# Attention by the two-level scheme of layer 1: exp(a) v as (exp(a) h) Wv^T in a graph-attention kernel

## The chip, the cores and the metric

The kernel runs on one core of one Trainium2 chip. The metric is the device time of one execution in microseconds, the median of several. A core has five engines, each with its own instruction queue: TensorE (PE, matrix products; its weight loads are listed as PEld), VectorE (DVE), ScalarE (ACT), GpSimd (POOL) and SyncE (SP), which here only issues loads. They meet through semaphores. Transfers run beside them; SP issues the loads and POOL the stores.

## The reference, cut to what matters

```python
h = maximum(layernorm(x), 0)                       # x: 3327 x 512, adj: 3327 x 3327
q, k, v = h @ Wq.T + bq, h @ Wk.T + bk, h @ Wv.T + bv
a = q @ k.T / sqrt(512) + adj + adj
x = x + softmax(a) @ v                             # layer 0
h = maximum(layernorm(x), 0)
A2 = adj + eye
temp = A2 @ h @ W.T
d = diagonal(A2) ** -0.5
out = x + relu((d[:, None] * A2 * d[None, :]) @ temp)   # layer 1
```

All of it is in fp32. So there are four large products: the scores, exp(a) with v, A2 with h, and A2 with temp. The rows are padded to 26 tiles of 128.

## The kernel before, in words

All large products are made by a recursive scheme of Strassen's kind (Winograd's form): a 2 x 2 block product in seven products instead of eight, with four sums of blocks of the left matrix (`four_sums`, L169) and four differences of the right one (`four_differences`, L175). The upper and lower half of the nodes are 13 tiles each (`HALF`); `STRIPS` and `HT` cut the columns into a strip of 2 x 7 tiles (s = 0) and one of 2 x 6 tiles (s = 1); the half widths `Q` are 448 and 384. On-chip memory is one arena of named slots (`large`, `mid`, `half`, `quarter`), which `ring` hands out in turn. A tile whose slot was used before waits until the last reader of the old one is done, a store's landing among them.

**Prologue.** M = Wq^T Wk is made on PE (L293). `h_transposed` (L309) normalises tiles of x, applies relu on ACT, transposes them on PE and keeps h^T with its sums in `hp`, four packs of 3, 3, 3 and 4 tile pairs (`PACKS`). `project_q` (L329) and `project_v` (L360) make q and v of a pack by one level of the scheme and store them in memory, POOL issuing. `Chain` (L223) writes the seven products of one level so that each partial result is evicted from its PSUM bank while others run; the last product, p4, of a chain runs after the fourth product (p6) of the next.

**Scores.** 52 steps: four groups of columns (strip s, half q), 13 tile pairs t in each. A step loads four quarter blocks of adj^T into `g` (`adjacency`, L428), runs a `Chain` of 28 PE records with DVE adding each product to 2 adj (`first`, `more`, L477 and L482), lets ACT take exp (`settle`, L470) and stores the four blocks of exp in `pd`. Beside the evictions `outer_sums` (L438) makes the next step's four sums of A2 = adj + 1 for layer 1 and stores them in `sumd`. `in_order` (L122) holds DVE, PE, POOL and SP to the order of the program text in this stage; elsewhere Tile's scheduler orders the instructions.

**Attention.** 91 units (L615 on): for two row tiles of the result at a time and each t, `weights` loads exp blocks, `four_sums` makes their sums, DVE adds up the row sums, and 7 x 2 products of width 256 with the blocks of v go into seven banks (L634). At t = 12 `attend` (L565) takes the row sums by small matmuls with `ones` (L573), puts the seven products together, divides, adds x, stores x1, normalises and stores h of layer 1 in `rowd`.

**Layer 1.** Two passes g = 0 and 1 (A2 with h, A2 with temp) by two levels of the scheme. The outer level is seven products in turn (`ORDER`: p5, p1, p6, p7, p2, p3, p4), each for two strips, in steps t = 0 to 5, which take two tile pairs each, and a last one with the odd tile (`t is None`). `left` (L720) loads the outer block or sum of A2 (from `adjT` or `sumd`), `sums` makes the four inner sums on DVE, `Right` loads and combines the right-hand rows (`load` 7 steps ahead, `make` 4 ahead), `multiply` (L798) issues 7 matmuls of width 448 or 384 (L810; L802 for the odd tile), and `gather` puts a product's result into `cts`. After a product's sums for a tile are complete, `temp` (L864, 4 matmuls of width 512, L869) multiplies with W, and `finish` writes the output. `between` names what else is put after which step. The five slots of `a_ring` let `left` run ahead.

Of the kernel before, what the change touches and what calls it, by code (L numbers as in the profile page):

```python
# [15 lines left out]
P = 128  # L16
# [28 lines left out]
def graph_layers_kernel(  # L45
# [26 lines left out]

    nc = tc.nc
# [30 lines left out]

    def quarter(k, shape, name):
        return arena.tile(shape, F32, name=name, tag=f"quarter{k}")
# [53 lines left out]

    qd = dram.tile([P, DC, NP], F32, name="qd")
    vd = [dram.tile([P, 4, E], F32, name=f"vd{t}") for t in range(HALF)]
    pd = [[dram.tile([P, 4, H[s]], F32, name=f"p{s}_{t}") for t in range(HALF)] for s in range(2)]
    sumd = [[dram.tile([P, len(SUMS), H[s]], F32, name=f"sum{s}_{t}") for t in range(HALF)] for s in range(2)]
    x1d = [dram.tile([P, D], F32, name=f"x1d{i}") for i in range(NT)]
    rowd = [[dram.tile([P, D], F32, name=f"row{g}_{i}") for i in range(NT)] for g in range(2)]
    t2d = [[dram.tile([P, 4, P], F32, name=f"t2{g}_{t}") for t in range(PAIRS + 1)] for g in range(2)]
# [38 lines left out]
    PACKS = ((0, 3), (3, 3), (6, 3), (9, 4))  # L206
# [55 lines left out]
    x_ring = ring(*((mid, k) for k in (0, 1, 2, 5)))  # L262
    v_ring = ring(*((mid, k) for k in (9, 10, 11, 12, 3, 6, 7, 8)))
# [5 lines left out]

    order = [(k, t + y * HALF) for k, (a, n) in enumerate(PACKS) for t in range(a, a + n) for y in range(2)]  # L270
    first = {i: load_x(i, nc.scalar) for _, i in order[:4]}
# [9 lines left out]
    bv_sb = quarter(0, [P, D], "bv_sb")  # L281
    nc.sync.dma_start(bv_sb, bass.AP(tensor=bv.tensor, offset=bv.offset, ap=[[0, P], [1, D]]))
    w_v = blocks(range(8, 12), "wv")
    for c in range(DC):
        for z in range(2):
            nc.sync.dma_start(w_v[2 * (c // 2) + z][:, c % 2], wvT[c * P : (c + 1) * P, z * E : (z + 1) * E])
# [17 lines left out]
    for b in (M, w_v):  # L304
        for _ in four_differences(b):
            pass
        nc.scalar.mul(b[0], b[0], -1.0)

    def h_transposed(k):  # L309

        a, n = PACKS[k]
        for _, i in (o for o in order if o[0] == k):
            xt = first.pop(i) if i in first else load_x(i)
            rstd, nb = norm(xt)
            nc.scalar.activation(xt, xt, AF.Relu, bias=nb, scale=rstd)
            pt = tp_bank("tp").rearrange("p (c e) -> p c e", c=DC)
            for c in range(DC):
                nc.tensor.transpose(pt[:, c], xt[:, c * P : (c + 1) * P], ident)  # L318
# [10 lines left out]
    def project_q(k):  # L329
# [3 lines left out]
        qs = [half(12 + j, [P, 2, BW], "qs") for j in range(4)]  # L333
# [26 lines left out]
    def project_v(k):  # L360
        a, n = PACKS[k]

        def chain(t0, m):
            vs = [v_ring([P, 2, E], "vs")[:, :m] for _ in range(4)]

            def product(ps, name, start):
                for j in range(m):
                    for c in range(2):
                        nc.tensor.matmul(ps[:, j * E : (j + 1) * E], h_of(t0 + j, name, c), w_v[B[name]][:, c],  # L369
                                         start=start and c == 0 and j == 0, stop=c == 1, skip_group_check=True)  # L370

            def of(ps):
                return ps[:, : m * E].rearrange("p (j e) -> p j e", j=m)

            def first(j, ps, sign):
                z = j % 2
                bias = bv_sb[:, z * E : (z + 1) * E].unsqueeze(1).to_broadcast([P, m, E])
                (nc.vector.tensor_add if sign > 0 else nc.vector.tensor_sub)(vs[j], bias, of(ps))

            def more(j, ps):  # L380
                nc.vector.tensor_add(vs[j], vs[j], of(ps))

            def last():
                for j in range(m):
                    for y in range(4):
                        nc.gpsimd.dma_start(vd[t0 + j][:, y], vs[y][:, j])

            Chain(product, first, more, last)

        for t0 in range(a, a + n, 2):  # L390
            chain(t0, min(2, a + n - t0))

    h_transposed(0)
    for k in range(len(PACKS)):
        if k + 1 < len(PACKS):
            h_transposed(k + 1)
        project_q(k)
        project_v(k)
# [4 lines left out]
    groups = [(s, q) for s in range(2) for q in range(2)]  # L403
    g_rings = ring(*((mid, k) for k in range(4))), ring(*((mid, k) for k in range(4, 9)))
    o_ring = ring(*((mid, k) for k in range(9, 13)))
    q_slots = ((0, 1, 2, 3, 4, 5, 6, 7), (8, 9, 10, 11, 12, 13, 14, 15))
# [31 lines left out]
    def outer_sums(s, q, t, g):  # L438

        wd, c = Q[s], q * Q[s]  # L440
        pair = [o_ring([P, 2, Q[0]], "o")[:, :, :wd] for _ in range(2)]
        o = [pair[m // 2][:, m % 2] for m in range(4)]
        of = ((g[0][:, 0], g[0][:, 1]), (g[1][:, 1], g[0][:, 1]), (o[1], g[0][:, 0]), (o[2], g[1][:, 0]))
        crossing = []
        for n, parts in enumerate(((0, 2, 3), (0, 1, 2, 3), (3,), (1, 2, 3))):
            k, y = divmod(n, 2)
            d = diagonal(o[0], (k * HALF + t) * P, STRIPS[s] * P + y * H[s] + c)
            crossing += [(m, d) for m in parts] if d else []
        for m in range(4):
            nc.vector.tensor_add(o[m], *of[m])  # L450
            yield
            if m % 2 and not crossing:
                nc.gpsimd.dma_start(sumd[s][t][:, m - 1 : m + 1, c : c + wd], pair[m // 2])
        for k, (m, d) in enumerate(sorted(crossing, key=lambda mark: mark[0])):
            nc.vector.tensor_add(o[m][:, d[0]], o[m][:, d[0]], d[1])
            if k % 2:
                yield
        for m in range(2) if crossing else ():
            nc.gpsimd.dma_start(sumd[s][t][:, 2 * m : 2 * m + 2, c : c + wd], pair[m])

    def scores(s, q, t, qt, g):
        wd, c = Q[s], q * Q[s]
        a = [g[0][:, 0], g[0][:, 1], g[1][:, 0], g[1][:, 1]]

        def product(ps, name, start):
            for k in range(2):
                nc.tensor.matmul(ps[:, :wd], h_of(t, name, k), qt[B[name]][:, k], start=start and k == 0, stop=k == 1,  # L467
                                 skip_group_check=True)

        def settle(k):  # L470
            if k == 1 and t == HALF - 1:
                nc.scalar.activation(g[k], g[k], AF.Exp, bias=pad)
            else:
                nc.scalar.activation(g[k], g[k], AF.Exp)  # L474
            nc.gpsimd.dma_start(pd[s][t][:, 2 * k : 2 * k + 2, c : c + wd], g[k])  # L475

        def first(n, ps, sign):  # L477
            nc.vector.scalar_tensor_tensor(a[n], a[n], 2.0, ps[:, :wd], op0=ALU.mult,  # L478
                                           op1=ALU.add if sign > 0 else ALU.subtract)
            next(beside, None)  # L480

        def more(n, ps):  # L482
            nc.vector.tensor_add(a[n], a[n], ps[:, :wd])
            if n == 1:
                settle(0)
            next(beside, None)
# [846 lines left out]
```

## Time and profile before

| | |
|---|---|
| time, median of 3 (range) | 2268.92 us (2268.39 to 2269.64) |
| span of the profiled execution | 2262.4 us |
| PE, DVE, ACT, POOL busy | 98%, 63%, 10%, 13% |
| transfers | 457.6 MB, 202 GB/s over the span |
| stages: prologue, scores, attention, layer 1 | 202, 515, 520, 1025 us |

The stages' borders are the first matmul of L467 at 202.1 us, the first after which only L634 runs at 717.2, and the first of layer 1 at 1236.9. Each fp32 matmul leaves two MATMUL records and two weight loads in the trace; the counts in the profile are of records. Among the groups of instructions, a row gives the line, engine and operation, the written and read tiles, their shapes and the number, then busy time and the mean duration of one, then the idle time of that engine just before. The costliest are L810 (2352 records), L634 (2366), L467 (1456). A duration of one matmul is longer than the distance to the next, because they overlap.

A row of the stage windows has the window's ends and length, the busy time of each engine with its instructions in brackets, the granted clock of PE, the mean busy share of the 16 DMA engines, and GB/s. In the time line a row has start, duration, engine, line and operation, and in brackets how long the engine was idle before and what ended that.

### The profile page before, as it was taken

Reading aid. Unit: us, or ns where it says so; the run is one execution under the profiler, and the core shown is the slowest. Engines: PE = TensorE matmul, PEld = TensorE weight load, DVE = VectorE, ACT = ScalarE, POOL = GpSimd, SP = SyncE. Lnnn points to the kernel's source line nnn. Section 1 sums busy time; section 2 is a strip of 40 time slices with the busy share of each in tenths; the row PEclk is TensorE's granted clock in tenths of the full one; section 3 lists DMA queues with packets and bytes.
Section 4 is the critical chain, followed back from the end, with each engine's and each line's share of the span. In section 5 each row is a group of like instructions: output and inputs, shape, how many; then the busy total and the mean of one; then the engine's idle time right before and its main releaser. Section 6 shows DMA issues by size and latency. Waiting matters only on the chain.

```text
span 2262.4 us, 22368 instructions
## 1 busy us (share of the span) xinstructions
PE 2220.2 (98%) x7522; PEld 1405.8 (62%) x7522; DVE 1431.7 (63%) x2935; ACT 227.5 (10%) x322; POOL 294.5 (13%) x462
## 2 busy tenths in 40 slices
PE   7999999999998999999999999999999999999996
PEld 4766555555555888888888555555545455555554
DVE  5445676767766565574666767777645357777774
ACT  4221111112111000000000000000000000000011
POOL 2323222233331011010110000000000000000001
PEclk9999999999999999999999999999999999999998
DMA  4435878887886344263454767666646467766684
GB/s 150 138 119 174 309 258 286 282 280 267 299 304 222 93 144 141 74 195 92 141 189 153 260 217 246 218 209 205 207 136 212 140 205 271 231 196 214 202 274 139
DMA packets 230412, 457.62 MB, mean 202 GB/s; under 512 B 25394, under 2 KB 135696, under 8 KB 230288
## 3 DMA queue, kind: packets, MB, share of 16 engines
q1 hardware_dynamic: 192464, 322.12, 45.9%
q0 software_dynamic: 37248, 132.93, 15.6%
q8 instruction: 61, 1.00, 0.2%
q10 hardware_dynamic: 576, 1.05, 0.1%
q14 instruction: 63, 0.52, 0.1%
HBM read 323.11 MB, written 132.90 MB: 202 GB/s over the span
## 4 chain that ended last, share of the span: by engine, by line
PE 87%; issue 7%; DMA 2%; DVE 2%; POOL 1%; SPq 0%; ACT 0%; POOLq 0%; DVEq 0%; ACTq 0%
PE p L810 33%; PE p L634 18%; PE Y L467 12%; PE Z L467 6%; PE p L869 4%; PE X L467 3%; PE p L802 3%; PE Y L369 2%; PE Y L338 2%; PE Z L369 1%; PE Z L338 1%; PE mm L293 1%; POOL out_dram L88 1%; PE X L369 0%; PE tp L318 0%
## 5 line engine op out<-in xcount | busy, mean ns | idle before, releaser
L810 PE MATMUL p<-part,b 128*128 128x448 f32 (+1 forms) x2352 | 834.0, 513 | 1.7 <-DVE b L178 0.9
L810 PEld LDWEIGHTS p<-part,b 128*128 128x128 f32 x2352 | 445.5, 190 | 371.9 <-issue 208.1
L634 PE MATMUL p<-vr,o 128*128 128x256 f32 x1352 | 322.0, 380 | 2.9 <-DVE vr L179 1.8
L467 PE MATMUL Y<-qt,hp 128*128 128x448 f32 (+1 forms) x832 | 308.4, 513 | 3.2 <-DVE g L478 3.0
L634 PEld LDWEIGHTS p<-vr,o 128*128 128x128 f32 x1352 | 257.0, 190 | 38.8 <-DVE vr L179 2.2
L171 DVE TENSOR_TENSOR part<-part 128x896 f32<-128x896 f32 (+1 forms) x168 | 171.6, 1022 | 162.2 <-PE p L810 104.3
L634 PE MATMUL p<-vr,pt 128*128 128x256 f32 x1014 | 250.5, 380 | 0.0
L467 PEld LDWEIGHTS Y<-qt,hp 128*128 128x128 f32 x832 | 157.8, 190 | 136.5 <-issue 73.3
L634 PEld LDWEIGHTS p<-vr,pt 128*128 128x128 f32 x1014 | 192.5, 190 | 26.0
L467 PE MATMUL Z<-qt,hp 128*128 128x448 f32 (+1 forms) x416 | 162.3, 513 | 0.0
L627 DVE TENSOR_TENSOR sums<-sums,pt 128x512 f32<-128x512 f32 (+1 forms) x84 | 54.7, 651 | 140.0 <-DMA pt<-p 139.9
L478 DVE SCALAR_TENSOR_TENSOR g<-g,Y 128x448 f32<-128x448 f32 (+1 forms) x156 | 91.6, 587 | 66.1 <-PE Y L467 64.4
L474 ACT ACTIVATE g<-g 128x896 f32<-128x896 f32 (+1 forms) x100 | 89.6, 896 | 410.1 <-DVE g L478 341.8
L467 PEld LDWEIGHTS Z<-qt,hp 128*128 128x128 f32 x416 | 79.2, 190 | 65.9 <-issue 38.6
L475 POOL DMA_DIRECT2D p<-g x104 | 75.5, 726 | 212.6 <-ACT g L474 204.7
L173 DVE TENSOR_TENSOR part<-part,part 128x384 f32<-128x384 f32 (+1 forms) x146 | 85.9, 589 | 9.0 <-PE p L810 0.5
L172 DVE TENSOR_TENSOR part<-part,part 128x384 f32<-128x384 f32 (+1 forms) x146 | 85.9, 589 | 3.1
L802 PE MATMUL p<-part,b 128*128 128x448 f32 (+1 forms) x224 | 82.8, 513 | 0.0
L467 PE MATMUL X<-qt,hp 128*128 128x448 f32 (+1 forms) x208 | 81.1, 513 | 0.0
L606 POOL DMA_DIRECT2D x1d<-xt x26 | 14.5, 558 | 454.1 <-DVE xt L605 443.7
L843 ACT COPY part<-p 128x448 f32<-128x448 f32 (+1 forms) x28 | 14.1, 505 | 588.6 <-PE p L810 558.2
L872 POOL DMA_DIRECT2D row<-ts x26 | 14.0, 539 | 435.2 <-ACT ts L871 435.2
(174 smaller groups left out, 1994.9 us busy)
## 6 DMA issues: line engine op xcount, KB each, us to landing
part<-sum SPq DMA_DIRECT2D x104, 448.0 KB, 4.7
pt<-p SPq DMA_DIRECT2D x78, 512.0 KB, 4.1
part<-sum SPq DMA_DIRECT2D x104, 384.0 KB, 3.5
part<-in_adjT_dram SPq DMA_DIRECT2D x78, 448.0 KB, 4.4
part<-in_adjT_dram SPq DMA_DIRECT2D x78, 384.0 KB, 3.6
g<-in_adjT_dram SPq DMA_DIRECT2D x52, 448.0 KB, 5.5
sum<-o POOLq DMA_DIRECT2D x52, 448.0 KB, 4.6
p<-g POOLq DMA_DIRECT2D x52, 448.0 KB, 3.4
```

The lines of the kernel that those rows point to most:

```text
L171: nc.vector.tensor_add(o[:, 0:2], g[:, 0:4:3], g[:, 1:2].to_broadcast([P, 2, g.shape[-1]]))
L172: nc.vector.tensor_add(o[:, 2], o[:, 1], g[:, 0])
L173: nc.vector.tensor_add(o[:, 3], o[:, 2], g[:, 2])
L338: nc.tensor.matmul(ps[:, :w], M[B[name]][:, c, o * P : (o + 1) * P], hp[k][:, A[name], c], start=start and c == 0, stop=c == 1, skip_group ...
L467: nc.tensor.matmul(ps[:, :wd], h_of(t, name, k), qt[B[name]][:, k], start=start and k == 0, stop=k == 1, skip_group_check=True)
L474: nc.scalar.activation(g[k], g[k], AF.Exp)
L475: nc.gpsimd.dma_start(pd[s][t][:, 2 * k : 2 * k + 2, c : c + wd], g[k])
L478: nc.vector.scalar_tensor_tensor(a[n], a[n], 2.0, ps[:, :wd], op0=ALU.mult, op1=ALU.add if sign > 0 else ALU.subtract)
L634: nc.tensor.matmul(ps[r][:, m * E : (m + 1) * E], a[:, m * P : (m + 1) * P], vr[t][:, b], start=t == 0 and m == 0, stop=t == HALF - 1, ski ...
L802: nc.tensor.matmul(ps[("p2", "p3", "p4", "p8")[k]][:, :w], b[:, z], a[:, 0, y], start=k == 3, stop=True)
L810: nc.tensor.matmul(ps[r][:, :w], b[:, i], m, start=self.t == 0, stop=self.t == PAIRS - 1 and r in ("p1", "p5", "p6", "p7"))
L869: nc.tensor.matmul(ps, cts[s][y][d][:, k * P : (k + 1) * P], w1[d], start=d == 0, stop=d == DC - 1)
```

## The change

Since v = h Wv^T + bv, and a row of softmax adds up to one, exp(a) v / rowsum = ((exp(a) h) Wv^T) / rowsum + bv. The change computes exp(a) h first, in the form of layer 1's product, and multiplies by Wv^T after it.

- v, `project_v`, the attention's own loop and its `attend` go. The prologue stores h (`rowd[0]`) and x + bv (`xbd`) for each tile instead. Pack 0 is now the one of four tile pairs, the packs are taken in the order 1, 2, 0, 3, and x, h and x + bv get rings of 7, 4 and 4 slots.
- Layer 1's code runs for three passes. In the new pass g = 0 `left` loads all seven blocks and sums of exp(a) from `pd`, and `attend` takes temp's place: product with Wv^T, division by the row sum and x + bv added in one DVE operation, x1 stored, norm, h of layer 1 stored.
- The scores' code makes the outer sums S1 to S4 of exp(a) (`s3`, `s1`, `s2`, `s4`, in the two steps after the exp) and adds up two halves of the row sums (`gather(m)`), which at each group's end are summed over the partitions by a matmul with `ones` and stored in `totd`.
- To make room on DVE, only two of the four sums of A2 are made there (S3 and S1). S2 and S4 are made from memory in 26 jobs each (`Job`), S2 beside the pass over exp(a), S4 beside the first pass over A2.

The sums of A2 that go, and what takes their place in the scores, with the order of the operations beside each eviction:

```diff
-        of = ((g[0][:, 0], g[0][:, 1]), (g[1][:, 1], g[0][:, 1]), (o[1], g[0][:, 0]), (o[2], g[1][:, 0]))
...
-        for m in range(4):
-            nc.vector.tensor_add(o[m], *of[m])
...
+    g_rings = ring(*((mid, k) for k in range(4))), ring(*((mid, k) for k in range(4, 8)))
...
+                beside[{0: 0, 3: 1, 1: 3, 2: 4}[n]]()
...
+                beside[{0: 2, 1: 5, 3: 6}[n]]()
...
+        def s4(self):
+            if self.t % 2 == 0:
+                Pair.fours = mid(12, [P, 2, Q[0]], "s4")
+            self.last = Pair.fours[:, self.t % 2, : self.wd]
+            nc.vector.tensor_add(self.last, self.e[:, 1], self.g[1][:, 0])
+            nc.gpsimd.dma_start(self.to(pd)[:, 6], self.last)
+
+        def gather(self, m):
+            if self.t == 0 and m == 0:
+                Pair.acc = acc_ring([P, 2, Q[0]], "acc")[:, :, : self.wd]
+            acc, new = Pair.acc, self.last if m else self.g[0][:, 1]
...
+                nc.vector.tensor_add(acc[:, m], acc[:, m], new)
...
+            ps = tp_bank("tot")
+            nc.tensor.matmul(ps[:1, : self.wd], ones, acc[:, m], start=True, stop=True)
...
+        return (
+            lambda: (on(k - 2, "s4"), on(k - 2, "gather", 0)),
+            lambda: (on(k - 1, "s3"), on(k - 2, "gather", 1)),
+            lambda: on(k + 1, "sum_of_adjacency", 0),
+            lambda: on(k + 1, "sum_of_adjacency", 1),
+            difference,
+            lambda: on(k - 1, "s1"),
+            lambda: on(k - 1, "s2"),
+        )
```

The prologue's two new stores, and the three passes with their additions:

```diff
-            nc.scalar.activation(xt, xt, AF.Relu, bias=nb, scale=rstd)
+            ht = n_ring([P, D], "ht")
+            nc.scalar.activation(ht, xt, AF.Relu, bias=nb, scale=rstd)
+            nc.gpsimd.dma_start(rowd[0][i], ht)
+            xb = xb_ring([P, D], "xb")
+            nc.vector.tensor_add(xb, xt, bv_sb)
+            nc.gpsimd.dma_start(xbd[i], xb)
...
+            if g == 0:
+                nc.sync.dma_start(a[:, k], pd[s][j][:, E_AT[what], :])
+                continue
...
+        def load(self):
+            w, r0, c0 = H[self.s], (self.k * HALF + self.j) * P, STRIPS[self.s] * P
+            self.a, self.b = (job_ring([P, H[0]], "job")[:, :w] for _ in range(2))
+            nc.sync.dma_start(self.a, sumd[self.s][self.j][:, self.at - 1])
+            nc.sync.dma_start(self.b, adjT[r0 : r0 + P, c0 : c0 + w])
...
+        def make(self):
+            nc.vector.tensor_add(self.a, self.a, self.b)
...
+            nc.gpsimd.dma_start(sumd[self.s][self.j][:, self.at], self.a)
...
+        ps = times_weights(i, wv_w1[0])
+        nc.vector.scalar_tensor_tensor(xt, ps, rs[:, i : i + 1], xt, op0=ALU.mult, op1=ALU.add)
+        nc.gpsimd.dma_start(x1d[i], xt)
+        rstd, nb = norm(xt)
...
+    for what, k0, k1 in (("S2", number_of(0, 0, 0, 3), number_of(0, 5, 0, 6)),
+                         ("S4", number_of(1, 0, 1, 4), number_of(1, 4, 1, 2))):
+        jobs = [Job(what, s, j) for s in range(2) for j in range(HALF)]
+        for n, job in enumerate(jobs):
+            k = k0 + n * (k1 - k0) // len(jobs)
+            at(k, job.load)
+            at(k + 1, job.make)
```

## The prediction, made before the change was run

> **What bounds the kernel now.** I read the page's busy times first, then the windows of the four stages, then the chain of waits in order of time. The page:
>
> ```profile
> PE 2220.2 (98%) x7522; PEld 1405.8 (62%) x7522; DVE 1431.7 (63%) x2935; ACT 227.5 (10%) x322; POOL 294.5 (13%) x462
> ```
>
> TensorE (PE) is busy throughout. The windows cut at the stages' borders (prologue, scores, attention, layer 1 in two halves; columns: PE, weight loads, DVE, ACT, POOL, clock, share of the DMA engines, GB/s) say whether that holds in each:
>
> ```profile
> 0.00:202.10 202.10, 189.00 (x748) 132.38 (x749) 98.59 (x242) 55.41 (x96) 57.58 (x98) 0.98 0.43 139
> 202.10:717.20 515.10, 511.90 (x1469) 278.78 (x1468) 352.79 (x689) 95.13 (x106) 151.93 (x212) 1.00 0.80 277
> 717.20:1236.90 519.70, 516.77 (x2415) 454.94 (x2413) 314.00 (x722) 22.72 (x30) 37.83 (x67) 1.00 0.44 137
> 1236.90:1740.00 503.10, 501.42 (x1410) 267.04 (x1411) 330.62 (x655) 21.22 (x34) 19.19 (x35) 1.00 0.66 212
> 1740.00:2262.40 522.40, 501.08 (x1487) 272.64 (x1485) 335.69 (x629) 33.04 (x56) 27.99 (x52) 0.98 0.65 209
> ```
>
> It does, but for 13 us of the prologue and the last 20. The second resource is not DVE (60 to 68%) but the transfers: 0.80 in the scores, where the kernel writes most. "Busy" hides a matmul's pitch, so I take that from the chain, where unbroken runs are listed with their record counts:
>
> ```profile
> 998.85 78.67 PE p L634 x364
> ...
> 1304.24 31.57 PE p L810 x84
> 1335.81 3.01 PE p L802 x8
> 1338.81 27.09 PE p L810 x84
> 1365.90 2.58 PE p L802 x8
> ```
>
> A record 256 wide costs 78.67/364 = 0.2161 us, 448 wide 31.57/84 = 0.3758, 384 wide 27.09/84 = 0.3225. Every matmul leaves two such records. Cost is in proportion to width (0.844, 0.839 and 0.840 ns a column), so wide tiles alone win nothing; only fewer columns do.
>
> **The Trainium skill.** "Perfetto Trace Analysis", section Identifying the Most-Contended Engine, says that matmul busy time is a poor measure of headroom because of pipelining; the trace agrees (the 256-wide records show 380 ns each and come every 216), hence the pitches. "VectorE: DVE Perf Modes", section The TRN2 errata, gives a fp32 two-input add as (N+151)/0.96 ns: 624 at 448; the trace has 619 to 622. "DMA: Bandwidth & Descriptors", section Issuing engines are not separate DMA queues: transfers from all issuers share the same 16 engines. So writes from POOL slow the loads from SP; no row of before isolates that. Its section Where 436 GB/s comes from puts the HBM side at about 358 GB/s; the trace is near: 325 GB/s at share 0.93 (below), or 349 at 1.
>
> **The change, part by part.**
>
> *Removed on PE.* The attention's 2366 records x 0.2161 = 511.3 us; its 52 row-sum matmuls, 0.79 us for 8 in the chain, 5.1; the v projection, 364 records of the same width, 78.7. Together 595.1.
>
> *Added on PE.* One more pass of layer 1's code: per product r, the four runs above, 64.25 us, times seven = 449.8. The product with Wv: 26 tiles x 4 matmuls x 2 = 208 records 512 wide, the same as temp in layer 1, which the chain holds at 3.9% of the span = 88.9. Row sums: 2 matmuls for each of 4 column groups, 2(0.752 + 0.645) x 2 = 5.6. Together 544.3. Net -50.8: this is the whole gain, and PE has to stay fed to get it.
>
> *Prologue.* Without v only the transposes, M and q are left. PE needs 202.1 - 77 = 125 until the scores if nothing else slips (1.7 us of the last v lay in the scores). Each x tile now costs DVE bn_stats 0.66, three small ones 0.4, the new x + bv add 0.6, and on every second tile two adds of 0.33: about 2.0 us, 12 for six tiles, and 5 for the pack's sums and q's evictions. One pack's q is 56 records x 0.3225 = 18.1 us of PE. DVE 17 against PE 18 plus transposes, where q and v together covered 36 before: PE will now wait here and there. Two more POOL stores a tile (0.55 each) hide: 26 x 1.7 = 44 us of about 100. I take +6 (0 to 15).
>
> *Scores, DVE.* Seven evictions stay. Four sums of A become two; four of exp(A) and two accumulations come in: 15 instead of 11. In the timeline such operations start 0.53 us apart when queued (470.28, 470.82), so 15 x 0.53 = 8.0, plus 0.3 for the query differences, in a step of 28 x 0.3758 = 10.5 us. DVE at 80% still fits; evictions have about two products (3 us) of slack before their bank is written again. Cost 0. The exps stay on ACT (95 us of 515).
>
> *Scores, row sums.* At each group's end gather issues a matmul in the middle of the chain, and the order of PE and DVE is written out. PE has done m1 and its next instruction is that matmul, which waits for three queued DVE operations: the eviction of m1, S4, the accumulation. From the timeline:
>
> ```profile
> 468.58 1.67 PE L467 MATMUL X<-qt,hp 128*128 128x448 f32 x4
> ...
> 470.08 3.17 PE L467 MATMUL Y<-qt,hp 128*128 128x448 f32 x8
> ...
> 470.28 0.62 DVE L483 TENSOR_TENSOR g<-g,X 128x448 f32<-128x448 f32 x1 [0.41 <-PE X L467]
> ```
>
> The eviction starts 0.2 us after the product; then 2 x 0.54 and the last one's 0.62: PE is idle about 2.0 us, and once more after p5 for the second half. Three borders between groups: 3 x 2 x 2.0 = +12. At the last border the sums wait at the end, and banks 6 and 7, which p5 and p2 of the next stage need, come free late; +2 over the 3 us lost there now.
>
> *Scores, transfers.* Per step 4 quarters in and 8 out become 4 in and 9 out: 277 x 13/12 = 300 GB/s. The g buffers of step k are now held until S4 and the accumulation early in step k+2; only then can the load for step k+4 start, whose first sum comes in step k+3: about one step (9 to 10.5 us) for a load that lands in 4.4 to 5.5 us now. Behind that sum on DVE are all evictions, so a late load would stop PE. I take 0 (to 15).
>
> *exp(A) times h.* All of exp(A)'s sums come from memory, so no diagonal adds. x + attention is evicted by DVE (0.69) where ACT evicts temp, then the norm, 1.85 us a tile, beside 8 us of PE: hidden.
>
> *S2 and S4 of A later.* 26 jobs for each, reading two tiles and writing one: 13 x (448 + 384) KB = 11.1 MB, times three = 33.2 MB. S2's are spread over 73 steps of 64.25/14 = 4.59 us, +99 GB/s; S4's over 54 steps, +134. One DVE add of about 1.0 us each hides in the 35% that is free, but it waits for its own load in DVE's queue, and the four sums for the next matmuls stand behind it. What the transfers have left is in layer 1's windows:
>
> ```profile
> 1320.00:1345.00 25.00, 25.00 (x71) 13.18 (x70) 13.24 (x21) 0.53 (x1) 0.00 (x0) 1.00 0.49 164
> 1345.00:1375.00 30.00, 30.00 (x91) 17.13 (x90) 23.95 (x50) 0.48 (x1) 2.38 (x5) 1.00 0.93 325
> 1375.00:1410.00 35.00, 35.00 (x98) 18.27 (x97) 23.97 (x42) 0.53 (x1) 0.86 (x2) 1.00 0.60 194
> 1410.00:1440.00 30.00, 30.00 (x91) 17.13 (x90) 24.14 (x51) 0.48 (x1) 0.00 (x0) 1.00 0.89 282
> ```
>
> Load comes in bursts (the rights of the next product are loaded in the second strip). Full rate is between 282/0.89 = 317 and 325/0.93 = 349. With S4's 134 the first burst wants 459, the second 416, the valleys 298 to 328: over the 215 us from 1285 on, 50 MB + 29 = 79 MB, or 226 us at 349 and 249 at 317: 11 to 34 us too much. Loads run about two steps ahead, which takes up some 3 MB (9 us). In the pass over exp(A), with 99, only the bursts exceed it. I take +9 for S4's stretch and +3 for S2's; bounds 0 and 49.
>
> **Sum.** -50.8 + 6 + 12 + 2 + 12 = -18.8: 2268.9 - 18.8 = 2250.
>
> **Rivals.** *A: the transfers are absorbed.* The scores stage already runs at 277 GB/s with PE idle for only 3 us; for it too: five buffers for the left tiles; against it: bursts at 0.93. Without the 12 for transfers and the 6 of the prologue: 2232. *B: transfers become the bound, slower than before.* At 317 GB/s, S4's stretch costs +33 and S2's (332 wanted over 335 us) +16, instead of 12: -50.8 + 20 + 49 = +18, 2287. For it: loads of 448 KB in layer 1 mostly run at 300 to 330 per full share; against it: 349 in the densest burst. *C: the scores are held by g's loads or DVE,* 0.3 us in each of 52 steps, +15: 2265, no change. Against it: one step of slack for 5.5 us.
>
> **Chances.** Mine 0.40, A 0.30, B 0.18, C 0.12. Faster by over 0.2% (under 2264.4): A and nearly all of mine, 0.69; within 0.2%: C and a rest of mine, 0.12; slower 0.19. The range goes from 2216, which is nearly the bare PE balance (2218), to 2285, which cuts into B.
>
> **What would show it.** Right: the prologue ends near 131; six PE gaps of about 2 us before matmuls of ones at group ends; the scores about 530 us; the exp(A) pass near 540; shares near 1 in S4's stretch, with PE waiting there for DVE sums that wait on loads. Wrong: PE never waiting on transfers (A), or PE waiting in every step of the scores (C) or through most of the S2 stretch (B).

## The result, and the profile after

| | before | after |
|---|---|---|
| time, median of 4 runs (range) | 2268.98 us (2268.39 to 2269.64) | 2305.12 us (2300.94 to 2310.54) |
| ratio to before, 95% interval | | 1.0161 (1.0139 to 1.0182) |
| PE busy / mean granted clock | 2220.2 us / 0.995 | 2205.0 us / 0.983 |
| transfers | 457.6 MB, 202 GB/s | 590.5 MB, 256 GB/s |

The changed kernel is 36 us slower, where the prediction had it 19 us faster. The page's busy times of the changed kernel first:

```profile
PE 2205.0 (96%) x6252; PEld 1170.6 (51%) x6252; DVE 1591.1 (69%) x3095; ACT 232.8 (10%) x336; POOL 361.7 (16%) x577
```

PE has 1270 records fewer, as the change intends, but is busy for only 15 us less and idle for 57 us more (2303.9 - 2205.0 = 98.9 against 42.2). The windows of the changed kernel, cut at its own borders (prologue, scores, the stretch with S2's jobs, one without jobs, the stretch with S4's jobs, the rest; columns as before), say where:

```profile
0.00:129.20 129.20, 112.37 (x388) 64.25 (x389) 75.67 (x204) 53.45 (x94) 60.69 (x99) 0.96 0.74 258
129.20:663.00 533.80, 518.83 (x1466) 277.39 (x1464) 433.44 (x829) 97.42 (x113) 178.11 (x258) 0.99 0.82 288
663.00:960.00 297.00, 273.81 (x748) 143.71 (x749) 210.38 (x403) 6.67 (x11) 23.84 (x42) 0.96 0.91 320
960.00:1311.00 351.00, 345.83 (x936) 177.90 (x935) 224.12 (x461) 25.20 (x34) 45.55 (x79) 1.00 0.66 216
1311.00:1560.00 249.00, 230.96 (x624) 119.31 (x624) 187.92 (x340) 3.03 (x6) 17.28 (x32) 0.97 0.92 331
1560.00:2303.90 743.90, 723.16 (x2097) 388.09 (x2095) 459.56 (x862) 47.01 (x78) 36.19 (x67) 0.99 0.63 202
```

The prologue ends at 129.2 us (131 forecast), the scores take 533.8 (530 forecast). So all of the miss lies after 663 us. There the two stretches with jobs stand out: PE is idle for 23.2 of 297 us and 18.0 of 249, the clock is 0.96 and 0.97, and the transfers are at 0.91 and 0.92 of their time. The stretch between them, with much the same PE work and two jobs' loads at its very end (1289 and 1300 us), has 5.2 us of idle time and clock 1.00.

The chain of waits of this profile goes back only to 2287 us, so it shows no matmuls to set beside those of before; the waits by engine take its place. PE's largest in the changed kernel (waits: engine, line and tile, what ended it; us in total, times, longest):

```profile
PE tot L495 <- DVE acc L490: 20.5, 7, 6.2
PE p L751 <- DVE part L785: 12.0, 6, 3.6
PE p L751 <- DVE part L789: 8.2, 6, 5.0
PE p L751 <- DVE ct L789: 7.2, 5, 3.1
```

The first row is the new row sums. The others, layer 1's matmuls behind `gather`, did not exist before: a late DVE. What DVE waits for is told by the queue of SP, in S2's stretch (690 to 960 us, waits of SP's queue):

```profile
SPq L815 <- DMA sum<-job: 53.4, 16, 7.5
SPq L665 <- PE p L751: 34.7, 33, 3.9
```

and in S4's (1311 to 1560 us):

```profile
SPq L815 <- DMA sum<-job: 68.4, 16, 7.7
SPq L672 <- PE p L751: 12.4, 11, 3.6
```

L815 is a job's first load, L665 and L672 are loads of left tiles. The left loads' own wait, for PE to be done with the tile before, is how a load that runs ahead should wait. The other is not: SP stands still 16 times in each stretch, for up to 7.7 us, until the *store* of an earlier job (`sum<-job`) has landed and its slot is free. SP takes its instructions in order, so the left tiles' loads behind it stand as well. The time line shows one such case. SP in the changed kernel (start, length from the first to the last of a group, line, transfer, number):

```profile
697.91 5.56 SPq L815 DMA_DIRECT2D job<-sum  x2
703.56 0.86 SPq L665 DMA_DIRECT2D part<-p  x2
705.72 2.45 SPq L816 DMA_DIRECT2D job<-in_adjT_dram  x2
708.26 0.94 SPq L665 DMA_DIRECT2D part<-p  x2
710.82 5.49 SPq L815 DMA_DIRECT2D job<-sum  x2
```

Two jobs' loads in a row hold the queue for 5.6 us, twice within 20 us. DVE and PE in the same time lines:

```profile
702.47 0.96 DVE L172 TENSOR_TENSOR part<-part 128x768 f32<-128x768 f32 x1 [5.68 <-DMA part<-p]
...
715.34 0.96 DVE L172 TENSOR_TENSOR part<-part 128x768 f32<-128x768 f32 x1 [2.77 <-DMA part<-p]
...
717.47 0.61 DVE L789 TENSOR_TENSOR ct<-part,p 128x448 f32<-128x448 f32 x1
```

```profile
718.14 0.91 PE L751 MATMUL p<-part,b 128*128 128x384 f32 x2 [3.13 <-DVE ct L789]
```

The left tile comes late; `four_sums` (L172) waits for it 2.77 us; the eviction L789 stands behind it in DVE's queue, although PE had finished all products issued so far by 715.0 us; PE needs that bank and is idle for 3.13 us. PE's idle time names DVE, and the cause stands two queues further back.

What brought the jobs' loads so close together: counted by the left tiles' loads between the first and the last job in SP's queue, S2's 26 jobs lie within some 43 steps, where the program text spreads them over 73, and S4's within some 44, where the text has 54. Tile's scheduler orders this stage, not the text. A job has two of the four job slots from its load to the landing of its store, so no more than two can be under way.

In the scores, at a group's end, the time line of PE shows the two waits that were forecast at 2.0 us:

```profile
260.61 0.80 PE L495 MATMUL tot<-acc,ones 128*1 128x384 f32 x2 [1.74 <-DVE acc L490]
261.35 1.77 PE L442 MATMUL Z<-qt,hp 128*128 128x448 f32 x4
264.93 0.80 PE L495 MATMUL tot<-acc,ones 128*1 128x384 f32 x2 [1.81 <-DVE acc L490]
```

### The profile page after: what moved, and what is told of

Read it like the earlier page. It is cut to its first block, busy times and chain, and to the rows that moved or that the text cites. A ratio compares the mean times of both kernels' runs of the same rounds, so it can differ in the third digit from the quotient of the medians.

```text
span 2303.9 us, 20984 instructions
## 1 busy us (share of the span) xinstructions
PE 2205.0 (96%) x6252; PEld 1170.6 (51%) x6252; DVE 1591.1 (69%) x3095; ACT 232.8 (10%) x336; POOL 361.7 (16%) x577
## 5 line engine op out<-in xcount | busy, mean ns | idle before, releaser
L751 PE MATMUL p<-part,b 128*128 128x448 f32 (+1 forms) x3528 | 1274.9, 519 | 34.0 <-DVE part L785 12.0
L751 PEld LDWEIGHTS p<-part,b 128*128 128x128 f32 x3528 | 672.3, 192 | 616.7 <-issue 321.8
L172 DVE TENSOR_TENSOR part<-part 128x896 f32<-128x896 f32 (+1 forms) x252 | 257.4, 1022 | 185.9 <-PE p L751 99.5
L442 PE MATMUL Z<-qt,hp 128*128 128x384 f32 (+1 forms) x416 | 162.5, 513 | 0.0
L174 DVE TENSOR_TENSOR part<-part,part 128x448 f32<-128x448 f32 (+1 forms) x219 | 128.9, 589 | 13.8 <-PE p L751 0.5
L173 DVE TENSOR_TENSOR part<-part,part 128x448 f32<-128x448 f32 (+1 forms) x219 | 128.8, 589 | 4.5
L829 PE MATMUL p<-w,ct 128*128 128x512 f32 x272 | 125.2, 600 | 3.3 <-DVE xt L837 3.3
L743 PE MATMUL p<-part,b 128*128 128x448 f32 (+1 forms) x336 | 124.5, 513 | 1.8 <-DVE xt L837 1.8
L446 DVE SCALAR_TENSOR_TENSOR g<-g,Y 128x384 f32<-128x384 f32 (+1 forms) x156 | 91.5, 586 | 29.3 <-PE Y L442 26.7
L820 DVE TENSOR_TENSOR job<-job 128x896 f32<-128x896 f32 (+1 forms) x52 | 53.2, 1022 | 63.0 <-DMA job<-in_adjT_dram 34.5
L743 PEld LDWEIGHTS p<-part,b 128*128 128x128 f32 x336 | 63.4, 190 | 55.7 <-issue 32.2
L829 PEld LDWEIGHTS p<-w,ct 128*128 128x128 f32 x272 | 52.1, 192 | 63.6 <-issue 52.9
L442 PE MATMUL X<-qt,hp 128*128 128x384 f32 (+1 forms) x208 | 83.9, 527 | 0.0
```

The costliest lines, as they stand in the source:

```text
L172: nc.vector.tensor_add(o[:, 0:2], g[:, 0:4:3], g[:, 1:2].to_broadcast([P, 2, g.shape[-1]]))
L173: nc.vector.tensor_add(o[:, 2], o[:, 1], g[:, 0])
L174: nc.vector.tensor_add(o[:, 3], o[:, 2], g[:, 2])
L442: nc.tensor.matmul(ps[:, :wd], h_of(self.t, name, k), qt[B[name]][:, k], start=start and k == 0, stop=k == 1, skip_group_check=True)
L743: nc.tensor.matmul(ps[("p2", "p3", "p4", "p8")[k]][:, :w], b[:, z], a[:, 0, y], start=k == 3, stop=True)
L751: nc.tensor.matmul(ps[r][:, :w], b[:, i], m, start=self.t == 0, stop=self.t == PAIRS - 1 and r in ("p1", "p5", "p6", "p7"))
```

## The experiments

The theory formed from the profile: the bunched jobs block SP's queue. The rivals: DVE's additions for the jobs, the transfers' rate, the half clock after PE's waits, the row sums. In this section "a stretch" is S2's (297 us from the end of the scores) or S4's (249 us), and the number of PE records in it is the yardstick: 0.351 us each where PE is fed (540.36 us busy for 1540 records in the first experiment). Every trace of the three-pass kernels holds the same 6252 records in all, so the counts can be set side by side.

### No jobs

```diff
-                nc.sync.dma_start(a[:, k], sumd[s][j][:, SUMS.index(what), :])
+                nc.sync.dma_start(a[:, k], sumd[s][j][:, {"S2": 1, "S4": 0}.get(what, SUMS.index(what)), :])
...
-        jobs = [Job(what, s, j) for s in range(2) for j in range(HALF)]
-        ...
+        pass
```

> The changed kernel without the 52 jobs: S2 and S4 of A2 are not made at all, and layer 1 loads S1 in place of S2 and S3 in place of S4, so its loads keep their number and size; the output is another function. In the trace of the changed kernel the stretch with S2's jobs (663 to 960 us) has 23 us of idle PE and the stretch with S4's (1311 to 1560) 18, and the granted clock drops to half after such gaps, some 20 us more in all. Theory 1 (the jobs' transfers, with the rest, exceed what the DMA engines carry) and theory 2 (a job's add, waiting for its load in DVE's queue, holds up the sums behind it): both about 2245, PE fed in both stretches. Theory 3 (the pass over exp(A) is slow of itself: its loads from pd, evictions by DVE): the first stretch keeps most of its idle time, 2275 or more.

Measured: 2245.29 us, ratio 0.9900 (0.9884 to 0.9917). The two stretches in the windows of this kernel:

```profile
663.00:960.00 297.00, 291.36 (x824) 155.78 (x823) 206.23 (x395) 5.51 (x10) 8.37 (x14) 0.99 0.68 225
1311.00:1560.00 249.00, 249.00 (x716) 135.78 (x715) 183.47 (x346) 4.04 (x8) 3.24 (x6) 1.00 0.68 221
```

The jobs cost 2305.1 - 2245.3 = 59.8 us. The stretches lost 824 - 748 = 76 and 716 - 624 = 92 records by them; 168 x 0.351 = 59 us, so the two stretches are the whole of it. Without jobs the forecast's sum is -18.8 - 12 = -30.8, or 2238 us; the measured time is 7 us from it. The rest of the forecast was thus about right, and the jobs are the error.

### Jobs without their additions

```diff
         def make(self):
-            nc.vector.tensor_add(self.a, self.a, self.b)
-            if self.d:
-                nc.vector.tensor_add(self.a[:, self.d[0]], self.a[:, self.d[0]], self.d[1])
             nc.gpsimd.dma_start(sumd[self.s][self.j][:, self.at], self.a)
```

> The jobs keep all their loads and stores, but no add is made: what was loaded from sumd is stored again, so S2 and S4 are wrong and DVE has nothing to do with a job. Theory 1 (transfers): within 10 us of the changed kernel, 2295 to 2310, with PE waiting for sums that wait for loads. Theory 2 (DVE's queue behind a job's load): near the run without jobs, 2245 to 2255.

Measured: 2314.35 us, ratio 1.0190 (1.0167 to 1.0213): not faster, though DVE has 52 additions less. In S2's stretch, the waits of SP and of DVE in this kernel:

```profile
SPq L815 <- DMA sum<-job: 69.5, 15, 7.8
```

```profile
DVE part L172 <- DMA part<-p: 67.3, 16, 9.7
```

SP's wait for slots is longer than in the changed kernel (53.4), and DVE, with less to do, waits 67.3 us for left tiles where it waited 19.8. So the loss needs none of the additions. What they cost by themselves the run doesn't tell, for it changed the order too: the scheduler put the jobs within some 32 and 39 steps (43 and 44 in the changed kernel), and some of their second loads into the scores, where SP waits for one before issuing the next (39.7 us from 560 to 672 us). Layer 1 starts at 673.5 us there, 9 us later than in the changed kernel (664.6).

### Jobs held to their place

A dependency that only orders, without a semaphore, keeps each job's first load behind the SP instruction that the text has before it.

```diff
+            traced = nc.cur_bb.bb.instructions
+            before = next(ins for ins in reversed(traced) if ins.engine == nc.sync.engine)
             nc.sync.dma_start(self.a, sumd[self.s][self.j][:, self.at - 1])
+            mine = next(ins for ins in reversed(traced) if ins.engine == nc.sync.engine)
+            tc.add_manual_dep(mine, before.name, ..., reason="in_order")
```

> Each job's first load is held in SP's queue behind the loads of the step that the program text names, so that S2's jobs take 73 steps and S4's 54; in the changed kernel the scheduler put them into 43 and 42 steps. Nothing else changes. Theory 1: the rate in S2's stretch falls from 321 GB/s to about 300 and its loss from some 35 us to 10 to 15, S4's loss from 26 to about 15: 2265 to 2280. Theory 2: each add still waits for its load; 2295 to 2305.

Measured: 2264.60 us, ratio 0.9973 (0.9959 to 0.9988), 40.5 us less than the changed kernel with the same work and the same bytes. Its windows:

```profile
663.00:960.00 297.00, 290.00 (x821) 154.94 (x820) 225.94 (x432) 6.66 (x11) 21.21 (x37) 0.99 0.90 317
1311.00:1560.00 249.00, 239.13 (x665) 126.44 (x664) 192.24 (x355) 4.04 (x8) 16.25 (x30) 0.98 0.91 327
```

Between the first and the last job's load lie 70 steps for S2 and 50 for S4. S2's stretch has 821 records, nearly as many as without jobs (824), at 317 GB/s. Its jobs now go on to 1006 us, 46 us into the stretch between, and that doesn't suffer: it has 937 records (936 in the changed kernel). SP's longest wait in S2's stretch is again the left tiles' own, and none is for a job slot's store:

```profile
SPq L665 <- PE p L751: 62.7, 48, 4.1
```

In S4's stretch, where the text itself puts the jobs closer (54 steps), SP still waits for job slots:

```profile
SPq L817 <- DMA sum<-job: 59.2, 12, 9.0
```

and there 51 records are missing, 51 x 0.351 = 18 us, which is what still separates this kernel from the one without jobs (19.3). This is the main result: the place of the jobs in the queues makes two thirds of their cost (40.5 of 59.8). The edit names SP's queue alone, but a job's addition and store follow its load. That the harm runs through SP's queue is read from the waits above and from the run without additions; no run moves the loads and leaves the rest.

### Row sums later

The matmuls with `ones` two products later, their results read later; the accumulation stays.

```diff
-            lambda: on(k + 1, "sum_of_adjacency", 0),
-            lambda: on(k + 1, "sum_of_adjacency", 1),
+            lambda: (on(k + 1, "sum_of_adjacency", 0), on(k - 2, "total", 0)),
+            lambda: (on(k + 1, "sum_of_adjacency", 1), on(k - 2, "total", 1)),
             difference,
-            lambda: on(k - 1, "s1"),
+            lambda: (on(k - 1, "s1"), on(k - 2, "store_total")),
```

> The two row-sum matmuls at a group's end are issued two products after the accumulation that they need, and read two products later; nothing else changes. If the six waits between groups are what their rows say (some 14 us idle, and half clock after two of them, 5 us): 2284 to 2290, and the scores 515 + 6 = 521 us. If the chain is held by DVE in any case, the waits move to the next evictions and the time stays above 2298.

Measured: 2290.44 us, ratio 1.0099 (1.0082 to 1.0117), 14.7 us less than the changed kernel. The six waits inside the scores, 14.3 us in the changed kernel, are gone; the one at the last border stayed (6.20 us there, 6.25 here). So it is about the forecast's +12 that this run won back, and the +2 is not part of it. The stretches with jobs are as bad as before (739 and 628 records).

### Both

```diff
+            tc.add_manual_dep(mine, before.name, ..., reason="in_order")
...
+            lambda: (on(k + 1, "sum_of_adjacency", 0), on(k - 2, "total", 0)),
```

> The two edits together: jobs held at their steps, and row-sum matmuls issued two products later. If the two losses are separate, their gains add: 2264.6 - (2305.1 - 2290.4) = 2250. If they share one cause (PE only waits elsewhere), 2260 or more.

Measured: 2245.70 us, ratio 0.9908 (0.9891 to 0.9924). The gains add up: 2305.1 - 40.5 - 14.7 = 2249.9. This kernel is faster than the one before by 0.9%. Its stretches lie 15 us earlier, since the scores are shorter:

```profile
648.00:945.00 297.00, 291.27 (x827) 155.97 (x826) 226.25 (x425) 5.51 (x10) 19.98 (x36) 0.99 0.91 319
...
1296.00:1545.00 249.00, 237.70 (x672) 127.33 (x671) 197.19 (x366) 3.51 (x7) 15.17 (x28) 0.99 0.92 328
```

S2's jobs now cost nothing; S4's still lack 716 - 672 = 44 records, 15 us.

### Gaps on PE, in the kernel before

The half clock by itself: 18 gaps of various lengths are put into the first pass of layer 1 of the kernel before, by a matmul that waits for a row of additions on DVE. The product is unchanged.

```diff
+            nc.vector.tensor_add(gap, ident, pg[:, P : 2 * P])
+            for _ in range(count):
+                nc.vector.tensor_add(gap, gap, ident)
+            nc.tensor.matmul(pg[:1, :P], ones, gap, start=True, stop=True)
```

> The kernel before, with 18 gaps on PE in layer 1's first pass, where it never waits and nothing else is short: after a step's matmuls a small matmul, then 2, 5, 9, 13, 17 or 25 adds of 128 on DVE that follow from it, then a small matmul of their result, and only then the next step; three gaps of each length, some 0.9, 1.6, 2.5, 3.3, 4.2 and 6 us. The output is the reference's. If an idle PE costs only its idle time: the sum of the gaps, 18 gaps or some 56 us, and the granted clock stays at 1.0. If a long gap is followed by half clock, as after the changed kernel's gaps: a stretch of 3.4 or 6.8 us at 0.5 after the longer ones only, 1.7 or 3.4 us more each, 70 to 85 us in all.

Measured: 2407.18 us, ratio 1.0615 (1.0596 to 1.0634). The gaps came out longer than meant, 0.95 to 11.54 us; the waits of PE give their sum:

```profile
PE p L977 <- DVE gap L976: 94.7, 18, 11.5
```

The span grew by 143.8 us, 49 more than the gaps. The windows of a gap of 6.98 us (1480.8 to 1487.8) and of the time behind it, then those behind one of 1.71 (1338.9 to 1340.6) and one of 2.99 (which ended at 1510.6):

```profile
1480.80:1487.80 7.00, 0.04 (x1) 0.04 (x2) 5.54 (x15) 0.00 (x0) 0.00 (x0) 0.72 0.80 259
1487.80:1490.80 3.00, 3.00 (x6) 1.56 (x7) 0.81 (x4) 0.48 (x1) 0.00 (x0) 0.51 0.29 88
1490.80:1497.00 6.20, 6.20 (x20) 3.61 (x19) 5.71 (x11) 0.00 (x0) 0.00 (x0) 1.00 0.38 103
...
1340.60:1344.00 3.40, 3.40 (x10) 1.71 (x11) 1.11 (x2) 0.53 (x1) 0.00 (x0) 1.00 0.45 127
...
1511.40:1514.80 3.40, 3.40 (x6) 1.62 (x5) 0.00 (x0) 0.00 (x0) 0.00 (x0) 0.52 0.34 97
```

After the long gap and after the one of 2.99 us PE runs at half clock for about 3 us (6 records where a fed PE does 10); after the one of 1.71 it doesn't. All 13 gaps from 2.99 us on were followed by 3.0 to 5.4 us at half clock, 1.5 to 2.7 us lost each, together about 30; none of the five up to 1.71 was. The rest of the 49, some 19 us, was not traced; the added small matmuls and what they delay are the likely part. The Trainium skill, "TensorE: Matmul & The Clock Gate", section HAM oscillation — how this bites in real kernels, warns of idle gaps over some 3.4 us; here 2.99 was enough, though a small matmul stands on either side of the gap, so that the large ones lie 3.5 us apart. A wait without such neighbours settles it: in the changed kernel one of 2.77 us (784.2 to 787.0) is followed by a clock of 0.51 from 787.6 to 794.5.

### Jobs spread over all steps

On top of both: the 52 jobs at equal distances over some 160 steps, not in the second strips of p1 and p6, with two slots of their own where the others are used.

```diff
+    jobs = [Job(what, s, j) for what in ("S2", "S4") for s in range(2) for j in range(HALF)]
+    crowded = {number_of(g, r, 1, t) for g in range(2) for r in (1, 2) for t in range(len(every))}
+    places = [k for k in range(3, number_of(1, 4, 1, 4)) if k not in crowded]
```

> As the run before, and all 52 jobs are spread over the steps from the first of the exp(A) pass to the fifth product of the next pass, also beside attend, but for the 28 steps of the second strips of p1 and p6, where the rights of the next product are loaded; beside attend a job has two slots of its own, and h of layer 1 keeps one slot instead of two. If what is left of the jobs' loss (some 7 us idle in the first stretch, 10 in the second, and half clock after two gaps) is crowding: 2238 to 2246. If the two slots or the single h slot hold SP or ACT up beside attend: 2250 or more.

Measured: 2247.36 us, ratio 0.9909 (0.9895 to 0.9924), no better than both alone (2245.70). The stretches are fed, S4's with 714 records, and SP's wait for job slots in it is down to 1.9 us (48.1 with both alone); but the stretch between them, now with jobs, has a new loss:

```profile
945.00:1296.00 351.00, 332.64 (x893) 169.94 (x892) 230.96 (x473) 24.43 (x33) 55.97 (x97) 0.99 0.82 282
```

It has 47 records fewer than with both alone (940), 16 us: there `attend` puts its own work on DVE, and PE waits for it (18 us behind L855). Jobs farther apart end the wait for slots, but this placing moved the loss and didn't remove it.

### Job loads from POOL

The changed kernel with the jobs' two loads issued by POOL, so that SP has only left tiles and rights.

```diff
-            nc.sync.dma_start(self.a, sumd[self.s][self.j][:, self.at - 1])
-            nc.sync.dma_start(self.b, adjT[r0 : r0 + P, c0 : c0 + w])
+            nc.gpsimd.dma_start(self.a, sumd[self.s][self.j][:, self.at - 1])
+            nc.gpsimd.dma_start(self.b, adjT[r0 : r0 + P, c0 : c0 + w])
```

> The changed kernel, with the jobs' loads issued from POOL instead of SP; they are not held, so they come as bunched as in the changed kernel, and the bytes are the same. Theory 1a (the bunched bytes exceed the transfers' rate): 2295 to 2315. Theory 1b (SP's queue: a job's load that waits for a job slot to be stored keeps the loads of the next left tiles behind it; SP waited 53 us for that in the first stretch and 68 in the second): 2265 to 2280.

Measured: 2352.76 us, ratio 1.0379 (1.0363 to 1.0396), outside all that was expected. The waits of this kernel, of POOL, DVE and PE:

```profile
POOL job L815 <- DMA sum<-job: 105.3, 41, 6.2
...
DVE job L820 <- DMA job<-sum: 90.1, 29, 7.4
...
PE p L751 <- DVE part L785: 54.1, 8, 11.6
```

The wait for slots has gone to POOL, and the jobs' additions, which stand in DVE's in-order queue, now wait for late job loads instead (90.1 us for these alone; in the changed kernel DVE was idle ahead of all jobs' additions for 63.0). Freeing SP alone doesn't help while the jobs stay bunched: DVE hands the wait to PE instead. Nor did they come merely as bunched as before, as was expected: they lie within some 30 and 32 steps here (43 and 44 in the changed kernel). So the run doesn't set the two queues side by side at equal order, and how much of the 48 us over the changed kernel is due to which was not traced further.

### More bytes, twice

To test the rate: on top of both, every job loads one more tile (52 loads, 22 MB), which nobody reads.

```diff
+            more = half(14, [P, H[0]], "more")[:, :w]
+            nc.sync.dma_start(more, adjT[r0 : r0 + P, c0 : c0 + w])
```

> The run with held jobs and later row sums (2245.7), and every job loads one more block of adj^T, which nobody reads, into a free slot: 11.1 MB more for S2's jobs and for S4's, so about 350 GB/s in their stretches instead of 315. If bytes are what the bunched jobs ran out of (theory 1a): 10 to 20 us slower, 2256 to 2266, with idle PE in both stretches. If it was the order and the waits for slots (the bytes being far from the limit): at most 4 us slower, under 2250.

Measured: 2303.78 us, ratio 1.0157 (1.0135 to 1.0178), but this doesn't answer the question. The loads were not held, and the scheduler put them into the scores, one waiting for the other in SP's queue ahead of the loads of `g`. SP and PE from 500 to 690 us:

```profile
SPq L835 <- DMA more<-in_adjT_dram: 128.9, 35, 7.0
```

```profile
PE Y L442 <- DVE g L446: 34.2, 12, 10.1
```

It shows the same mechanism once more, in another stage. Then with the added load held behind the job's own:

```diff
+            tc.add_manual_dep(third, mine.name, ..., reason="in_order")
```

> As the run with more bytes, but the extra load, too, is held behind its job's first load; in that run the scheduler had put the extra loads, for which nothing waits, into the scores (480 to 796 us), where each waited in SP's queue for the one before (129 us) with the loads of g behind it. Here they come one a job. With 11.1 MB more in each stretch the rates should rise from 315 to about 345 GB/s. If bytes alone were the limit that the changed kernel met (321 and 331 GB/s with PE starved): 10 to 30 us over 2245.7. If order and slots were: under 2252.

Measured: 2238.78 us, ratio 0.9877 (0.9859 to 0.9895). Its stretches:

```profile
648.00:945.00 297.00, 290.33 (x823) 155.15 (x822) 223.87 (x422) 5.52 (x10) 19.52 (x35) 0.99 0.96 350
...
1296.00:1545.00 249.00, 244.10 (x698) 131.16 (x697) 207.14 (x380) 4.05 (x8) 15.66 (x29) 1.00 1.00 374
```

With 22 MB more, at 350 and 374 GB/s, PE is fed better than in the changed kernel at 320 and 331. So the mean rate of a stretch was not what held the changed kernel.

In shorter pieces the changed kernel, too, reaches a share of 1: 0.99 to 1.01 from 1340 to 1430 us, at 347 to 376 GB/s, with 6.3 us of idle PE in 90. But this kernel has 1.00 to 1.04 and 367 to 403 GB/s from 1296 to 1445 us, with 3.9 us in 149. In S2's stretch PE stops where the DMA engines have time left, as in the changed kernel, and goes on where they have none, as in the kernel with held jobs:

```profile
840.00:880.00 40.00, 34.64 (x89) 17.72 (x88) 22.54 (x32) 0.53 (x1) 3.78 (x7) 0.91 0.93 323
...
800.00:840.00 40.00, 40.00 (x111) 20.90 (x110) 33.53 (x63) 1.01 (x2) 3.99 (x8) 1.00 1.03 399
```

That the kernel with more bytes is even 7 us faster than with both alone (2235.87 to 2242.45 against 2243.14 to 2249.60, in different sets of runs; the intervals of the ratios, 0.9859 to 0.9895 and 0.9891 to 0.9924, just overlap) goes with a shorter wait of SP for job slots in S4's stretch (35.9 us against 48.1): the added load stands between jobs and so keeps them apart. That last step is argued, not shown. It is the fastest kernel of the study: 1.2% faster than before, 2.9% than the changed one.

### Jobs out of the crowded strips

On top of both: no jobs in the second strips of p1 and p6, and so closer together elsewhere.

```diff
+            places = [k for k in range(k0, k1) if k not in crowded]
+            k = places[n * len(places) // len(jobs)]
```

> The run with held jobs and later row sums, with no job in the second strips of p1 and p6, where the rights of the next product are loaded; the jobs keep their ranges and slots and stand closer in the other steps (2.3 steps for S2, 1.5 for S4). If these crowded passes hold what is left of the loss: 2236 to 2242. If the closer jobs wait for their slots in the other passes: 2248 to 2260.

Measured: 2261.35 us, ratio 0.9974 (0.9960 to 0.9988), 15.7 us slower than with both alone. S4's stretch:

```profile
1296.00:1545.00 249.00, 232.37 (x628) 121.45 (x627) 185.34 (x337) 3.57 (x7) 15.67 (x29) 0.95 0.89 315
```

628 records instead of 672, at a lower rate and at clock 0.95. So keeping out of the bursts of the rights was worth less than distance between jobs; a limit of rate should have shown the other way, but that is argued. Nor is the wait for slots longer in S4's stretch here (42.9 us, 48.1 with both alone), so it doesn't explain this run by itself.

### The stretches together

PE records in each stretch, of the kernels with the same row sums side by side:

| kernel | S2's stretch | S4's stretch | time, us |
|---|---|---|---|
| changed | 748 | 624 | 2305.1 |
| no additions | 719 | 656 | 2314.4 |
| held | 821 | 665 | 2264.6 |
| no jobs | 824 | 716 | 2245.3 |
| row sums later | 739 | 628 | 2290.4 |
| and held (both) | 827 | 672 | 2245.7 |
| and out of the crowded strips | 814 | 628 | 2261.4 |
| and more bytes, held | 823 | 698 | 2238.8 |

## Why the prediction was wrong

- **Net PE balance, -50.8:** right in effect. Without jobs the kernel came to 2245.3 where the remaining terms give 2238. That checks their sum and not each.
- **Prologue, +6:** right. The scores start at 129.2 us (131 forecast).
- **Scores, DVE and transfers, 0:** right. DVE is busy 433.4 of 533.8 us, 81% (80% forecast); DVE waits 1.6 us in all for the loads of `g`, at 288 GB/s, and PE for none. Rival C did not occur.
- **Row sums, +12 and +2:** the +12 is right in size, and its mechanism holds for five of the six inner waits (1.72 to 1.81 us, 2.0 forecast). The sixth, 5.46 us, has another part: an operation of layer 1 (L713), which the scheduler put into DVE's queue there, waits 4.04 us for its own load. Moving the matmuls won 14.7. The +2 has the wrong reason: in the wait of 6.2 us at the last border DVE stands 5.74 us (to 678.3 us) until the store of an earlier S4 has landed and its slot is free; late banks are not what PE waits for.
- **Jobs, +12, "bounds 0 and 49":** wrong; 59.8 us, beyond the bound. The step that failed is "S2's are spread over 73 steps of 64.25/14 = 4.59 us, +99 GB/s; S4's over 54 steps". It took places in the program text for places in the queues, although the same document says that outside the scores Tile's scheduler orders the instructions. They came within some 43 and 44 steps. And it costed the jobs as bytes against a rate, although the jobs also need slots: two jobs under way, each until its store has landed, and the next one's load waiting *in SP's queue*, ahead of the left tiles. The prediction named what stands behind a job's addition in DVE's queue; it did not ask the same of its load on SP. That was the question which would have found it. Held to the forecast's places the jobs cost 2264.6 - 2245.3 = 19.3 us; that this is near the +12 is luck, for it is 3 records in S2's stretch and 51 in S4's, and, by the run with more bytes held, not the rate.
- **The rate:** "Full rate is between 282/0.89 = 317 and 325/0.93 = 349" was wrong too: 374 GB/s in the window above. A faster rate could have been read from the kernel before: 407 GB/s from 230 to 240 us, at a share of 1.03. The Trainium skill ("DMA: Bandwidth & Descriptors", section Where 436 GB/s comes from) has about 358 for the HBM side, as one core's half of what a stack gives; here one core runs alone, and its 374 goes past that. That 349 came near 358 was chance. The rate divided by the busy share of a half-loaded window is not the rate at full load.
- **Rival B** had the sign, but its mechanism, transfers as the bound, fell with the last experiment on bytes. "shares near 1 in S4's stretch", announced as a sign that the forecast was right, was seen (0.92), with PE behind late sums, and told nothing of the cause.
- **A term that was missing, the half clock.** The mean granted clock went from 0.995 to 0.983, 11 and 39 us of clock time over the two spans; without jobs it is 0.992 (18 us). The longest of PE's waits behind the jobs are 3.1 to 5.0 us, lengths which the gaps experiment shows to be followed by the half clock. Of the jobs' 59.8 us, idle time makes about 36 (41.2 idle in the two stretches, against 5.6 without jobs), and the clock, 0.03 lower in both (546 x 0.03), about 16; some of that lies in the idle time.

What stays open: why S4's stretch still lacks 44 records when jobs are held. The wait for slots points there: SP's wait and the stretch's records are 68.4 us and 624 in the changed kernel, 59.2 and 665 held, 48.1 and 672 with both, 35.9 and 698 with more bytes held, 1.9 and 714 with the jobs spread. But the run out of the crowded strips doesn't fit (42.9 and 628), and no run gave these jobs more slots alone. Open, too, is the size of the loss with loads from POOL.

## What to carry to other kernels

Ask of a background load the same as of a wait: in which in-order queue does it stand, what must be free for it to start, and what is behind it; where a scheduler orders the program, the place in the text answers none of that, and a dependency that only orders can hold the load to its place (40 us here, without one byte less). Count the slots: jobs per time is slots divided by the time from load to landed store, and what goes beyond that waits in the queue. A wait of TensorE of 3 us or more cost 1.5 to 2.7 us on top at half clock in the gaps run, and small matmuls that need a late result are better issued some products later.

## What the runs showed of the hardware that was not expected

- In the gaps run the half clock follows every gap of 2.99 us and more, and no gap of 1.71 or less (18 gaps). In the other traces the border is not sharp: a single wait of 2.25 us (row sums later, at 767.9 us) was followed by a clock of 0.50 from 769.3 to 776.1, one of 3.21 (loads from POOL, at 1232.9) by 1.00. Pairs of waits of 1.7 to 1.8 us, some 4.4 us apart, stand at the first two borders of the scores in each of five traces (changed, no jobs, no additions, held, from POOL). After five of these ten the clock is 0.50 for 3.4 us or more, in the changed kernel from 408.8 to 412.2. So waits close together seem to add up at times; what decides was not tested.
- Transfers went on at 374 GB/s over 249 us beside a TensorE that was fed 98% of the time, where the kernel before shows more than 349 only in windows of 10 us (up to 407).
- Twenty-two MB of loads that nobody needs made the kernel no slower, and by the runs some 7 us faster.
